# A row-wise LSTM behind a group norm: the second row's first products moved into the statistics, and the rest of it merged with the first row of the other half

## The chip, the cores and the metric

The kernel runs on one core of one Trainium2 chip. A core has five engines that each work through a queue of their own in order and wait for one another by semaphores: TensorE (PE in the profile, its weight loads PEld), VectorE (DVE), ScalarE (ACT), GpSimd (POOL) and SyncE (SP), which issues the transfers here. The metric is the time of one launch on the device in microseconds (us), taken as the median over several runs.

## The reference

The input `x` is an image batch of shape (8, 96, 128, 128): 8 images, 96 channels, 128 rows of 128 columns. It is normalised by group norm, 32 groups of 3 channels, with a mean and a variance over a whole image. A masked convolution of width 3 along each row gives 384 gate inputs. Then an LSTM runs down the 128 rows, where the state of a row is itself convolved along the columns:

```python
xn  = gn(x)                                    # mean and variance per image and group
its = conv1x3(xn, W_is * mask) + b_is          # for all rows
for row in range(128):
    gates = conv3(h, W_ss) + b_ss + its[row]
    f, i, o, g = sigmoid, sigmoid, sigmoid, tanh of the gates' quarters
    c = f * c + i * g
    h = o * tanh(c)
    out[row] = x[row] + h
```

The state before the first row is zero, so the first row needs no forget gate.

## The kernel before

**Two stages.** First the statistics: `x` is streamed through a ring of six buffers, image by image, six loads of 1 MB for each and 24 pieces of 512 columns in all. VectorE takes the statistics of most pieces (`bn_stats`, line 741), ScalarE sums the others with two activations each (lines 216 and 217). A table `events` says what else is queued after which piece: `at(6, 17)` is after the piece with number 17 of image 6. Then comes the recurrence, which nothing but the order of the rows binds.

**Halves and half-steps.** The batch is cut in two halves of four images, s = 0 and s = 1, so that one half's matmuls cover the other's gates. A half-step n handles row n // 2 of half n % 2; half-step 0 is row 0 of the first half, 1 is row 0 of the second, 2 is row 1 of the first. The images of the first half are scaled when their statistics are in, at `at(4, 5)`; half-step 0 runs inside the statistics of images 5 and 6. The second half's last image ends the statistics, so half-step 1 can begin only after them.

**One half-step.** Even and odd columns are kept apart, and the products are arranged so that the two outputs come out of sums and differences. The three gate tiles A, B and C have a bank of the matmul accumulator each (`ps`), two halves of 256 columns in it. The names in the order tables mean:

- `1` and `2`: matmuls of 128 contracted rows with the sum `vs` and the difference `vf` of the state's columns; `0` and `3`: the same with `vd`, the shifted differences
- `P`, `Q`, `E` (method `own`): matmuls of 64 contracted rows with the row's own image channels `xs`. The operands lie twice, in partitions 0 to 63 and 64 to 127; `low` picks one, by gate tile
- `cp` copies the first half of the bank with the bias added (`m`, lines 424 and 426); `lo` and `hi` write sum and difference back into the bank (lines 429 and 433). `E` and `0` then add to the first half, `3` to the second
- `ta`, `si`: tanh and sigmoid on ScalarE (lines 436 and 443); `fg`, `gt`, `ce`, `th`, `ou`: forget product, gate product, cell sum, tanh of the cell, output (lines 448, 452, 461, 466, 473)
- `F`, `S` on VectorE (lines 490 and 486) and `D` on GpSimd (line 494) make `vf`, `vs` and `vd` of the next row; `re` adds the output to `x` on GpSimd (line 512)

All matmuls of a half-step stand at line 380. A mark behind a name shifts it: `'` is the half-step before, `+` the next, `*` the one after that.

**What sets the order.** Every engine's queue is written out by hand. `do(n, names)` issues the named parts in order; `PERIOD` and `PRODUCTS` are the order of a half-step in the long run. `finish(n)` issues what comes up for later rows: own images of the next four rows (`own_image`, lines 292, 310 and 311 on GpSimd), shared channels (`normalise_shared`), loads of rows (`load_rows`, `load`) and stores. For half-steps 0 to 7 the list `FIRST` says which. Eight banks of the accumulator go round in the order of their request (`bank`), and a request waits until the last reader of the bank it gets is done.

**Fillers.** `spin(count, rhs)` issues matmuls whose result nobody reads, into a bank of their own; `keep_warm(count)` is one small one, tied to a piece of the statistics, and `count` more. `Scale` turns statistics into scale and shift by small matmuls (line 246) and a polynomial on VectorE; the second half has two, one for three images and one for the last (`late[1]`), each with two banks, `dm` and `pv`.

Behind the statistics, lines 746 to 786 scale the last image and make `vs`, `vf` and `vd` of half-step 1, then rows 1 to 3 of the second half's own images (`rows`, made by GpSimd one row after the other). The end of it and the start of the long run:

```python
    do(1, "1A 2A 1B 2B PA PB QA QB PC P+A QC")
    for n in range(1, last + 1):
        for names in PERIOD if n < last else PERIOD[:1]:
            do(n, PRODUCTS[n % 2] if names == "X" else names)
```

Of the kernel before, what the change touches and what calls it, by code (L numbers as in the profile page):

```python
# [21 lines left out]
def kernel(  # L22
# [34 lines left out]
    P = 128  # L57
    NH = 2
# [112 lines left out]
    def spin(count, rhs):  # L171
        unread = bank("spin")
        for i in range(count):
            nc.tensor.matmul(
                unread[:, 0 : rhs.shape[1]],
                wt[0][:, 0:P],
                rhs,
                start=True,
                stop=True,
                skip_group_check=True,  # L180
            )
# [44 lines left out]
    class Scale:  # L226


        def __init__(self, s, lo, hi):
            n, self.name = hi - lo, f"{s}_{lo}"  # L230
            self.st, self.rstd, self.nmr = (
                st[s][:, lo:hi], rstd[s][:, :, lo:hi], nmr[s][:, :, lo:hi]
            )

            self.dm = bank(f"dm{self.name}")[:, 0 : 3 * n].rearrange("p (i b) -> p i b", i=3)
            self.pv = bank(f"pv{self.name}")[:, 0 : 2 * n].rearrange("p (i b) -> p i b", i=2)
            self.pm = self.dm[:, 1:3, :]
            self.q, self.t, self.minus = (
                const.tile([P, *shape], F32, name=f"{name}{self.name}")
                for name, shape in (("q", [n]), ("t", [2, n]), ("minus", [2, n]))  # L240
            )
            for i in range(2):
                self.mm(self.pv[:, i, :], i, eps[:, 0:n], start=i == 0)

# [3 lines left out]
        def deviations(self):  # L248
            self.mm(self.dm[:, 0, :], 2, self.st[:, :, 0], start=True)

# [106 lines left out]
    class HalfStep:  # L357


        def __init__(self, n):  # L360
            self.row, self.s = divmod(n, NH)
            self.ps, self.m1, self.moving, self.done, self.gates = {}, {}, {}, set(), None
            self.hx = hx[self.s][self.row // R % 2][:, self.row % R]
            self.xs = xs[self.s][self.row // R % 2][:, self.row % R]
            self.c = cs[self.s].rearrange("p t b j -> p (t b j)")
# [5 lines left out]
        def g(self):  # L371
            if self.gates is None:
                self.gates = self.tile("g")
            return self.gates

        def mm(self, a, half, weights, rhs, rows=slice(0, P)):
            new = a not in self.ps
            if new:
                self.ps[a] = bank(f"ps{a}_{self.s}_{self.row}")
            nc.tensor.matmul(  # L380
                self.ps[a][:, bass.ts(half, HB)],
                weights[rows, bass.ts(a, P)],
                rhs[rows],
                start=new,
                stop=False,
                skip_group_check=True,
            )

        def own(self, a, i):

            low = a == order["A"] or (a == order["C"] and self.s == 0)
            rhs = self.xs[:, i].rearrange("p b j -> p (b j)")
            self.mm(a, i % 2, wo[i], rhs, slice(0, C2) if low else slice(C2, P))
# [26 lines left out]
        def copy(self, a):  # L420
            self.m1[a] = self.tile(f"m{a}", (P, HB))
            m1, column = self.ps[a][:, 0:HB], bias[:, a : a + 1]
            if a == order["A"] and self.row + self.s > 0:
                nc.vector.tensor_scalar(self.m1[a], m1, column, None, ALU.add)
            else:
                nc.scalar.activation(self.m1[a], m1, AF.Identity, bias=column)  # L426
# [101 lines left out]
    def shared(s, k, *images):  # L528
        return [(normalise_shared, nc.gpsimd, s, k, j, 0, R) for j in images]

    FIRST = [
        own(0, 0) + shared(0, 1, 0),
        own(0, 1, 2),
        own(0, 3) + [(load_rows, 0, 2)] + shared(0, 1, 1),
        own(1, 0, 1),
        own(1, 2) + shared(0, 1, 2, 3),
        own(1, 3) + [(load_rows, 1, 2)] + shared(1, 1, 0, 1),
        [(own_image, 0, 2, 0)] + shared(1, 1, 2, 3),
        [(own_image, 1, 2, 0)],
    ]  # L540
# [124 lines left out]

    def begin_scale(s, lo, hi):
        late.insert(0, Scale(s, lo, hi))
        late[0].deviations()
        late[0].variances(late[0].st[:, :, 1])
# [6 lines left out]
    def keep_warm(count):  # L676
# [7 lines left out]
        at(3, 21): lambda: first_rows(0, (2,)),  # L684
        at(4, 5): lambda: begin_scale(0, 0, BH),
        at(4, 6): squares,
# [9 lines left out]
        at(6, 8): lambda: (do(0, "gt th ou"), operands(2), do(0, "re")),  # L696
        at(6, 22): lambda: first_rows(1),
        at(7, 5): lambda: (late.insert(0, Scale(1, BH - 1, BH)), begin_scale(1, 0, BH - 1)),
        at(6, 17): lambda: keep_warm(13),
        at(7, 7): squares,  # L700
# [71 lines left out]
    step.total(lo=BH - 1)  # L772
    step.difference(lo=BH - 1)
    widen(nc.scalar, xw[1], BH - 1, 1, 1, 0, BH - 1, 0)
    own_row(xw[1], 1, 0, BH - 1, BH)
# [12 lines left out]

    do(1, "1A 2A 1B 2B PA PB QA QB PC P+A QC")
    for n in range(1, last + 1):  # L790
        for names in PERIOD if n < last else PERIOD[:1]:
            do(n, PRODUCTS[n % 2] if names == "X" else names)
            if "re'" in names.split():
                finish(n - 1)
# [66 lines left out]
```

## Time and profile before

| what | value |
|---|---|
| median of 4 runs | 2067.07 us (2066.55 to 2067.77) |
| profiled execution | 2065.83 us, its span 2064.0 us |
| busy: PE, DVE, ACT, POOL | 95%, 81%, 66%, 70% of the span |
| granted clock of TensorE, mean | 0.996 |
| matmuls at line 380, 128 rows: mean of one | 380 to 388 ns |
| copies (L426), sums (L429), differences (L433): mean of one | 474, 424, 429 ns |
| own images on POOL: L292, L311: mean of one | 806, 1062 ns |
| last input statistics on VectorE end | 132.4 us |

The page gives the busy time of each engine, then the span in 40 slices with a digit for each (tenths of the slice), then the chain of work that ended last, followed back from the end. Groups and timelines give the engine, the line, the operation, what it writes from what it reads, and in brackets how long the engine was idle before and what ended that. An f32 matmul shows as two records. The number in the clock's column is the share of full speed that TensorE was granted.

### The profile page before, as it was taken

Reading aid. Unit: us, or ns where it says so; the run is one execution under the profiler, and the core shown is the slowest. Engines: PE = TensorE matmul, PEld = TensorE weight load, DVE = VectorE, ACT = ScalarE, POOL = GpSimd, SP = SyncE. Lnnn points to the kernel's source line nnn. Section 1 sums busy time; section 2 is a strip of 40 time slices with the busy share of each in tenths; the row PEclk is TensorE's granted clock in tenths of the full one; section 3 lists DMA queues with packets and bytes.
Section 4 is the critical chain, followed back from the end, with each engine's and each line's share of the span. In section 5 each row is a group of like instructions: output and inputs, shape, how many; then the busy total and the mean of one; then the engine's idle time right before and its main releaser. Section 6 shows DMA issues by size and latency. Waiting matters only on the chain.

```text
span 2064.0 us, 31433 instructions
## 1 busy us (share of the span) xinstructions
PE 1961.5 (95%) x10880; PEld 1598.1 (77%) x10880; DVE 1677.8 (81%) x3490; ACT 1362.3 (66%) x2402; POOL 1446.3 (70%) x1652
## 2 busy tenths in 40 slices
PE   0389999999999999999999999999999999999998
PEld 0268888888888888888888888888888888888886
DVE  5768888888888888888888888888888888888887
ACT  4776666666666666666666666666666666666666
POOL 3358777777777777777777777777777777777762
PEclk9989999999999999999999999999999999999999
DMA  9994333444333344433334443333444333344411
GB/s 384 424 308 103 77 85 86 112 112 113 93 77 85 87 110 113 113 93 77 86 86 110 113 113 93 77 87 87 108 112 113 95 75 88 87 107 113 113 31 31
DMA packets 103325, 236.26 MB, mean 114 GB/s; under 512 B 5952, under 2 KB 8896, under 8 KB 97280
## 3 DMA queue, kind: packets, MB, share of 16 engines
q1 hardware_dynamic: 103168, 234.25, 41.2%
q8 instruction: 88, 1.44, 0.3%
q14 instruction: 69, 0.57, 0.1%
HBM read 183.90 MB, written 50.33 MB: 113 GB/s over the span
## 4 chain that ended last, share of the span: by engine, by line
PE 93%; DMA 3%; DVE 2%; ACT 1%; POOL 0%; issue 0%; SPq 0%; DVEq 0%; POOLq 0%
PE ps L380 93%; DMA xs<-in_x_dram 3%; DVE bst L741 1%; POOL xw L292 0%; POOL xs L311 0%; SPq L729 0%; POOL xs L310 0%; ACT piece L216 0%; ACT xs L216 0%; ACT xs L217 0%; ACT piece L217 0%; ACT g L436 0%; DVE st L664 0%; ACT th L466 0%; ACT ps L443 0%
## 5 line engine op out<-in xcount | busy, mean ns | idle before, releaser
L380 PE MATMUL ps<-vd,wl 128*128 128x256 f32 x3072 | 815.1, 388 | 0.0
L436 ACT ACTIVATE g<-ps 32x512 f32<-32x512 f32 x768 | 453.7, 591 | 453.4 <-PE ps L380 445.1
L380 PEld LDWEIGHTS ps<-vd,wl 128*128 128x128 f32 x3072 | 562.4, 190 | 151.2 <-issue 85.2
L494 POOL TENSOR_TENSOR vd<-hx 128x512 f32<-128x512 f32 x257 | 266.2, 1036 | 468.1 <-DVE vs L486 463.9
L380 PE MATMUL ps<-xs,wx 64*128 64x256 f32 x3072 | 457.7, 394 | 10.7 <-POOL xs L310 10.7
L380 PE MATMUL ps<-vs,wm 128*128 128x256 f32 x1536 | 458.6, 380 | 0.2 <-DVE vf L490 0.2
L380 PE MATMUL ps<-vf,wm 128*128 128x256 f32 x1536 | 458.2, 380 | 0.0
L443 ACT ACTIVATE ps<-ps 96x512 f32<-96x512 f32 x766 | 417.5, 572 | 16.2
L380 PEld LDWEIGHTS ps<-xs,wx 64*128 64x128 f32 x3072 | 322.8, 187 | 119.0 <-issue 84.2
L448 DVE TENSOR_TENSOR ps<-ps,c 96x512 f32<-96x512 f32 x254 | 176.8, 696 | 260.9 <-ACT ps L443 260.9
L433 DVE TENSOR_TENSOR ps<-m,ps 128x256 f32<-128x256 f32 x768 | 329.5, 429 | 26.4
L512 POOL TENSOR_TENSOR x<-x,hx 96x512 f32<-96x512 f32 x255 | 330.1, 1294 | 5.7 <-DVE hx L473 5.7
L429 DVE TENSOR_TENSOR ps<-m,ps 128x256 f32<-128x256 f32 x768 | 325.7, 424 | 10.0 <-ACT m L426 1.2
L380 PEld LDWEIGHTS ps<-vs,wm 128*128 128x128 f32 x1536 | 292.4, 191 | 41.3 <-POOL vs L486 0.7
L380 PEld LDWEIGHTS ps<-vf,wm 128*128 128x128 f32 x1536 | 292.6, 191 | 40.4 <-DVE vf L490 0.3
L426 ACT ACTIVATE m<-ps,wl 128x256 f32<-128x256 f32 x513 | 243.2, 474 | 76.2 <-PE ps L380 62.5
L311 POOL TENSOR_TENSOR xs<-xw 128x512 f32<-128x512 f32 (+1 forms) x254 | 269.7, 1062 | 0.0
L380 PE MATMUL ps<-xs,wt 64*128 64x256 f32 x1530 | 263.3, 376 | 0.0
L466 ACT ACTIVATE th<-c 96x512 f32<-96x512 f32 (+1 forms) x257 | 161.4, 628 | 105.1 <-DVE c L461 104.3
L292 POOL TENSOR_SCALAR hx<-x,rstd,nmr 32x512 f32<-32x512 f32 (+1 forms) x252 | 203.7, 808 | 26.0
L380 PEld LDWEIGHTS ps<-xs,wt 64*128 64x128 f32 x1530 | 194.4, 187 | 18.0 <-issue 0.7
L292 POOL TENSOR_SCALAR xw<-xr,rstd,nmr 128x512 f32<-128x512 f32 x252 | 203.2, 806 | 7.1 <-DVE nmr L284 6.6
(91 smaller groups left out, 1303.3 us busy)
## 6 DMA issues: line engine op xcount, KB each, us to landing
xr<-in_x_dram SPq DMA_DIRECT2D x124, 512.0 KB, 6.4
x<-in_x_dram SPq DMA_DIRECT2D x63, 768.0 KB, 5.9
out_dram<-x SPq DMA_DIRECT2D x62, 768.0 KB, 4.6
xs<-in_x_dram SPq DMA_DIRECT2D x30, 1024.0 KB, 12.3
piece<-in_x_dram SPq DMA_DIRECT2D x16, 1024.0 KB, 12.3
x<-in_x_dram SPq DMA_DIRECT2D x62, 256.0 KB, 3.2
xs<-in_x_dram SPq DMA_DIRECT2D x4, 512.0 KB, 8.2
out_dram<-x SPq DMA_DIRECT2D x2, 576.0 KB, 3.8
```

The lines of the kernel that those rows point to most:

```text
L292: engine.tensor_scalar(dst, src, scale, shift, ALU.mult, ALU.add)
L311: nc.gpsimd.tensor_sub(differences, strided(xw[:, 0, :], 0, [(W + 1, n), (J, 2), (1, J)]), strided(xw[:, 0, :], J + 1, [(W + 1, n), (0, 2) ...
L380: nc.tensor.matmul(self.ps[a][:, bass.ts(half, HB)], weights[rows, bass.ts(a, P)], rhs[rows], start=new, stop=False, skip_group_check=True,)
L426: nc.scalar.activation(self.m1[a], m1, AF.Identity, bias=column)
L429: nc.vector.tensor_add(self.ps[a][:, 0:HB], self.m1[a], self.ps[a][:, HB:])
L433: nc.vector.tensor_sub(hi, self.m1[a], hi)
L436: nc.scalar.activation(self.g[a * 32 : (a + 1) * 32], self.ps[a][C:P], AF.Tanh)
L443: nc.scalar.activation(gate, gate, AF.Sigmoid)
L448: nc.vector.tensor_mul(f, f, self.c)
L466: nc.scalar.activation(self.part(self.th, lo, hi), self.part(self.c, lo, hi), AF.Tanh)
L494: diff = nc.gpsimd.tensor_sub(self.operand("vd", 2)[:, :, lo:hi], strided(h, 1, [(BH * JP - 1, 2), (JP, hi - lo), (1, J)]), strided(h, 0, ...
L512: (nc.gpsimd if 2 * row + s < last else nc.vector).tensor_add(xo, xo, self.h)
```

## The change

Half-step 2 (row 1 of the first half) is taken apart.

- Its products `P`, `Q`, `1` and `2` for all gate tiles are issued at a new event `at(6, 9)`, inside the statistics, and its three copies on ScalarE at `at(6, 22)`. Its sums and differences `lo` and `hi` are issued on VectorE behind the last image's scaling.
- What is left of it (`E`, `0`, `3`, gates, output) is merged with half-step 1: the 64-row matmuls of both, and the first ones of half-step 3, form one phase in which the low and the high operands alternate; then come `0` and `3` of half-step 1, then those of half-step 2. For half-step 1, `hi` is issued behind `E`. The long run begins at half-step 3.
- `at(6, 17)` has 6 filler matmuls instead of 13. Fillers use a bank of half-step 1, which is requested early (`take_bank`), and the two `Scale` objects of the second half share one pair of banks and are created at `at(6, 9)`.
- For half-step 1, `low` of gate tile C's `E` is changed, and half-step 2's copy of tile A is done on ScalarE.
- `FIRST` is dealt out anew: the shared channels and the third block's loads and images come one half-step later or so.

```diff
@@ -169,7 +169,7 @@
     def spin(count, rhs):
-        unread = bank("spin")
+        unread = half_step(1).ps[0]
         for i in range(count):
             nc.tensor.matmul(
                 unread[:, 0 : rhs.shape[1]],
@@ -226,27 +226,32 @@
     class Scale:
-        def __init__(self, s, lo, hi):
+        def __init__(self, s, lo, hi, banks=None):
             n, self.name = hi - lo, f"{s}_{lo}"
             self.st, self.rstd, self.nmr = (
                 st[s][:, lo:hi], rstd[s][:, :, lo:hi], nmr[s][:, :, lo:hi]
             )
-            self.dm = bank(f"dm{self.name}")[:, 0 : 3 * n].rearrange("p (i b) -> p i b", i=3)
-            self.pv = bank(f"pv{self.name}")[:, 0 : 2 * n].rearrange("p (i b) -> p i b", i=2)
+
+            self.first, at = banks is None, 0 if banks is None else 3 * BH
+            self.banks = banks or [bank(f"{name}{self.name}") for name in ("dm", "pv")]
+            self.dm, self.pv = (
+                own[:, at : at + i * n].rearrange("p (i b) -> p i b", i=i)
+                for own, i in zip(self.banks, (3, 2))
+            )
             self.pm = self.dm[:, 1:3, :]
             self.q, self.t, self.minus = (
                 const.tile([P, *shape], F32, name=f"{name}{self.name}")
                 for name, shape in (("q", [n]), ("t", [2, n]), ("minus", [2, n]))
             )
             for i in range(2):
-                self.mm(self.pv[:, i, :], i, eps[:, 0:n], start=i == 0)
+                self.mm(self.pv[:, i, :], i, eps[:, 0:n], start=self.first and i == 0)
         def mm(self, o, i, rhs, start=False, stop=False):
             nc.tensor.matmul(o, gm[:, i, :], rhs, start=start, stop=stop, skip_group_check=True)
         def deviations(self):
-            self.mm(self.dm[:, 0, :], 2, self.st[:, :, 0], start=True)
+            self.mm(self.dm[:, 0, :], 2, self.st[:, :, 0], start=self.first)
         def variances(self, of):
             for i in range(2):
@@ -358,8 +363,9 @@
         def __init__(self, n):
-            self.row, self.s = divmod(n, NH)
+            self.n, (self.row, self.s) = n, divmod(n, NH)
             self.ps, self.m1, self.moving, self.done, self.gates = {}, {}, {}, set(), None
+            self.started = set()
             self.hx = hx[self.s][self.row // R % 2][:, self.row % R]
             self.xs = xs[self.s][self.row // R % 2][:, self.row % R]
             self.c = cs[self.s].rearrange("p t b j -> p (t b j)")
@@ -373,10 +379,14 @@
                 self.gates = self.tile("g")
             return self.gates
+        def take_bank(self, a):
+            if a not in self.ps:
+                self.ps[a] = bank(f"ps{a}_{self.s}_{self.row}")
+
         def mm(self, a, half, weights, rhs, rows=slice(0, P)):
-            new = a not in self.ps
-            if new:
-                self.ps[a] = bank(f"ps{a}_{self.s}_{self.row}")
+            self.take_bank(a)
+            new = a not in self.started
+            self.started.add(a)
             nc.tensor.matmul(
                 self.ps[a][:, bass.ts(half, HB)],
                 weights[rows, bass.ts(a, P)],
@@ -388,7 +398,7 @@
         def own(self, a, i):
-            low = a == order["A"] or (a == order["C"] and self.s == 0)
+            low = a == order["A"] or (a == order["C"] and (self.s == 0 or (self.n, i) == (1, 2)))
             rhs = self.xs[:, i].rearrange("p b j -> p (b j)")
             self.mm(a, i % 2, wo[i], rhs, slice(0, C2) if low else slice(C2, P))
@@ -420,7 +430,7 @@
         def copy(self, a):
             self.m1[a] = self.tile(f"m{a}", (P, HB))
             m1, column = self.ps[a][:, 0:HB], bias[:, a : a + 1]
-            if a == order["A"] and self.row + self.s > 0:
+            if a == order["A"] and self.n not in (0, 2):
                 nc.vector.tensor_scalar(self.m1[a], m1, column, None, ALU.add)
             else:
                 nc.scalar.activation(self.m1[a], m1, AF.Identity, bias=column)
@@ -529,14 +539,14 @@
         return [(normalise_shared, nc.gpsimd, s, k, j, 0, R) for j in images]
     FIRST = [
-        own(0, 0) + shared(0, 1, 0),
-        own(0, 1, 2),
-        own(0, 3) + [(load_rows, 0, 2)] + shared(0, 1, 1),
+        own(0, 0),
+        own(0, 1),
+        own(0, 2) + shared(0, 1, 0, 1),
+        own(0, 3) + [(load_rows, 0, 2)] + shared(0, 1, 2, 3),
         own(1, 0, 1),
-        own(1, 2) + shared(0, 1, 2, 3),
-        own(1, 3) + [(load_rows, 1, 2)] + shared(1, 1, 0, 1),
-        [(own_image, 0, 2, 0)] + shared(1, 1, 2, 3),
-        [(own_image, 1, 2, 0)],
+        own(1, 2) + shared(1, 1, 0, 1),
+        own(1, 3) + [(load_rows, 1, 2)] + shared(1, 1, 2, 3),
+        [(own_image, 0, 2, 0), (own_image, 1, 2, 0)],
     ]
     def work(n):
@@ -663,8 +673,16 @@
     def aggregate(b):
         nc.vector.bn_aggr(st[b // BH][:, b % BH, :], stats[b])
-    def begin_scale(s, lo, hi):
-        late.insert(0, Scale(s, lo, hi))
+    def next_products():
+
+
+        late[0:0] = [Scale(1, 0, BH - 1)]
+        late.insert(1, Scale(1, BH - 1, BH, late[0].banks))
+        for a in range(3):
+            half_step(1).take_bank(a)
+        do(2, "PA PB QA QB PC QC 1A 2A 1B 2B 1C 2C")
+
+    def begin_scale():
         late[0].deviations()
         late[0].variances(late[0].st[:, :, 1])
@@ -682,7 +700,7 @@
         at(3, 1): lambda: first_rows(0, (0,)),
         at(3, 13): lambda: first_rows(0, (1,)),
         at(3, 21): lambda: first_rows(0, (2,)),
-        at(4, 5): lambda: begin_scale(0, 0, BH),
+        at(4, 5): lambda: (late.insert(0, Scale(0, 0, BH)), begin_scale()),
         at(4, 6): squares,
         at(4, 8): lambda: (
             late[0].scale(), late[0].shift(), [own_image(0, 0, j) for j in range(BH)]
@@ -694,9 +712,10 @@
             0, "loA hiA EA 0A 3A loB hiB EB 0B 3B loC hiC EC 0C 3C taA taB siB taC siC"
         ),
         at(6, 8): lambda: (do(0, "gt th ou"), operands(2), do(0, "re")),
-        at(6, 22): lambda: first_rows(1),
-        at(7, 5): lambda: (late.insert(0, Scale(1, BH - 1, BH)), begin_scale(1, 0, BH - 1)),
-        at(6, 17): lambda: keep_warm(13),
+        at(6, 9): next_products,
+        at(6, 17): lambda: keep_warm(6),
+        at(6, 22): lambda: (first_rows(1), do(2, "cpA cpB cpC")),
+        at(7, 5): begin_scale,
         at(7, 7): squares,
         at(7, 8): lambda: (next_row(), spin(14, wt[0][:, 0:256])),
         at(7, 12): next_operands,
@@ -771,6 +790,7 @@
     step = half_step(1)
     step.total(lo=BH - 1)
     step.difference(lo=BH - 1)
+    do(2, "loA loC loB hiA hiB hiC")
     widen(nc.scalar, xw[1], BH - 1, 1, 1, 0, BH - 1, 0)
     own_row(xw[1], 1, 0, BH - 1, BH)
     step.shifted(BH - 1, BH)
@@ -786,8 +806,14 @@
     load_rows(1, 1)
-    do(1, "1A 2A 1B 2B PA PB QA QB PC P+A QC")
-    for n in range(1, last + 1):
+
+    do(1, "1A 2A 1B 2B 1C 2C PA PB QA QB E+A PC E+C QC P*A E+B cpA cpB cpC loA loB loC")
+    do(1, "EA P*B Q*A EB EC Q*B hiA hiB hiC 0A 3A 0B 3B 0C 3C taA taB siB taC siC")
+    finish(0)
+    do(1, "gt th 0+A 3+A 0+B 3+B 0+C 3+C ou F S D re")
+    finish(1)
+    do(2, "taA siA P+C P*A Q+C")
+    for n in range(3, last + 1):
         for names in PERIOD if n < last else PERIOD[:1]:
             do(n, PRODUCTS[n % 2] if names == "X" else names)
             if "re'" in names.split():
```

## The prediction, made before the changed kernel was run

> **What bounds the kernel now.** I read the page first (slices, then the chain that ended last), then the chain in order of time around the change, then each engine's timeline from 84 to 185 us. A "full" matmul below contracts 128 rows, a "half" one 64; the timeline counts two records for each.
>
> ```profile
> PE   0389999999999999999999999999999999999998
> PE 93%; DMA 3%; DVE 2%; ACT 1%; POOL 0%; issue 0%; SPq 0%; DVEq 0%; POOLq 0%
> ```
>
> From the third slice on TensorE is never free, and 93% of the span hangs on it. Whatever is taken out of TensorE's queue after the statistics shortens the kernel by its own length, if nothing then makes TensorE wait. The chain says where that stretch begins:
>
> ```profile
> 115.39 2.01 ACT xs L217 x2
> 117.42 11.21 DMA xs<-in_x_dram
> 128.65 3.79 DVE bst L741 x6
> ...
> 133.31 0.35 PE dm L246 x2
> ...
> 137.08 92.99 PE ps L380 x519
> ```
>
> Up to 137.08 the order is: ScalarE frees a buffer, the last load lands at 128.6, VectorE takes its statistics, the last image is scaled. From 137.08 it is matmuls alone. The unit prices stand in TensorE's timeline of the two rows after that:
>
> ```profile
> 137.08 0.67 PE L380 MATMUL ps<-vs,wm 128*128 128x256 f32 x2 [0.15 <-DVE vf L490]
> 138.98 2.00 PE L380 MATMUL ps<-xs,wx 64*128 64x256 f32 x14
> 140.91 0.70 PE L380 MATMUL ps<-vs,wm 128*128 128x256 f32 x2
> ...
> 145.19 0.70 PE L380 MATMUL ps<-vd,wl 128*128 128x256 f32 x2
> ...
> 150.57 1.57 PE L380 MATMUL ps<-xs,wx 64*128 64x256 f32 x12
> ...
> 153.46 0.59 PE L380 MATMUL ps<-vf,wm 128*128 128x256 f32 x2
> ...
> 160.77 0.59 PE L380 MATMUL ps<-vf,wm 128*128 128x256 f32 x2
> ```
>
> A full matmul starts every 0.433 us. The twelve between 145.19 and 150.57 take 5.38, so a run of full ones costs 0.433 each plus 0.18. Halves on opposite row halves run side by side: eight fill 143.26 to 145.19 (1.93) and ten fill 150.57 to 152.93 (2.36), so a run costs 0.433 per pair plus 0.2. Half-step 4 (third row of the first half) begins at 160.77, 23.69 us after 137.08. From half-step 4 on TensorE, ScalarE and VectorE have the same instructions in the same order and with the same waits before and after the change. So the question is how long those 23.69 us become, and whether 137.08 moves.
>
> **The change, part by part.**
>
> *Products of half-step 2 inside the statistics.* Six half and six full matmuls leave the stretch behind 137.08. The halves need row 1's own images, ready at 90.5, and start behind half-step 0's last matmul at 103.8. The full ones need `vs`, which GpSimd has ready at 110.47. At the slow pace that the timeline shows at 93.40 to 98.69 (0.86 each) they end by 115.7. The seven spins that go and the `eps` matmuls lay off the chain, on an engine that idled 8.8 us before them.
>
> *Copies on ScalarE.* Three of 0.47 us (group of L426) go behind the first rows, which end at 119.19. The next instruction waits 1.58 us for a load there:
>
> ```profile
> 120.77 0.20 ACT L215 ACTIVATE base<-xs 128x1 f32<-128x1 f32 x1 [1.58 <-DMA xs<-in_x_dram]
> ```
>
> 1.4 us fit into 1.58, and their matmuls are done 3.5 us earlier: cost 0. Without that cover each microsecond would delay the last image's sums and so 137.08. ScalarE's release of the last buffers (117.2) stands ahead of all this and stays.
>
> *Sums and differences on VectorE.* Six of 0.43 us move from between half-steps to 137.07, where VectorE idles 3.07 us until 140.14. At a pitch of 0.34 to 0.46 they end by 139.5: cost 0. Their reader, the `E` products of half-step 2, starts at 140.7.
>
> *The 64-row phase.* TensorE's new order behind 137.08, by the unit prices:
>
> - 6 full (half-step 1): 2.6 + 0.17 = 2.77, to 139.85
> - 16 halves, 8 pairs: 3.46 + 0.2 = 3.66, to 143.5 without a wait
> - 12 full (half-steps 1 and 2): 5.38
> - 3 halves, 2 slots: 1.07
> - 9 full (half-step 3): 3.9 + 0.17 = 4.07
> - 8 halves, then 1 full: 1.93 + 0.53
>
> Sum 19.4 against 23.69: 4.3 us at most. Now the waits that appear.
>
> First wait: the ninth half is the first product of half-step 3, which was at 150.57 and would now be at 139.85 + 4 x 0.433 = 141.6. It reads row 1's own images, which GpSimd makes with nothing free before them:
>
> ```profile
> 138.30 3.06 POOL L292 TENSOR_SCALAR hx<-x,rstd,nmr 32x384 f32<-32x384 f32 x4
> 141.44 0.64 POOL L310 TENSOR_TENSOR xs<-piece 128x256 f32<-128x256 f32 x1
> 142.04 1.06 POOL L311 TENSOR_TENSOR xs<-piece 128x512 f32<-128x512 f32 x1
> ```
>
> So it starts at 142.1 (+0.5), and the thirteenth, which needs L311, at 143.15 (+0.2). Behind it, in order, wait the `E` products of half-step 1, on which its differences on VectorE now wait (they were ahead of `E` before); these end at 143.6, 144.2 and 144.6, each ahead of its matmul. The 12 full ones start at 144.2 instead of 143.5: 0.7 lost.
>
> Second wait: half-step 3 needs half-step 1's output, through its gates. The sixth full matmul ends at 144.2 + 5 x 0.433 + 0.59 = 146.96; tanh 0.59 behind the sigmoid that ends at 147.3, the gate product 0.69, tanh 0.63, output 0.69 and difference 0.43, with 0.04 between each, end at 150.45. TensorE arrives at 144.2 + 5.38 + 1.07 = 150.65: no wait, with 0.2 to spare.
>
> Third wait: half-step 3 holds 9 full matmuls ahead of its halves where it held 11 and one more behind, because two of half-step 2's are done already. TensorE reaches half-step 4 after 4.07 + 1.93 + 0.53 = 6.53 us, at 157.2. VectorE's queue from its first copy to the difference took 154.53 to 160.53 = 6.0 us, of which the last 0.83 is a difference that took 0.43 elsewhere; now it starts at 151.65 and ends between 157.25 and 157.65. I take 157.3, since GpSimd has nothing to run at that moment. Later half-steps have 7.3 to 7.7 us each, so the lead is kept.
>
> 160.77 - 157.3 = 3.5 us gained.
>
> *Shared rows, images and loads put off by a half-step or so.* GpSimd waited 2.97 us at 152.76 and 0.76 at 161.01, and the busiest half-step now asks 1.04 + 1.29 + 5.1 = 7.4 of 7.5 us. The issues of the third block's rows on the sync queue go one half-step later, with some 30 us until the first reader. Cost 0; a block that came late would cost what TensorE then waits.
>
> *Does 137.08 move?* Earlier: no. VectorE's 1.0 us wait at 122.89 for TensorE goes, but a load ends its next wait at 126.15, and another lands at 128.6. Later: by the granted clock (the first number behind the five engines).
>
> ```profile
> 105.00:106.00 1.00, 0.00 (x0) 0.00 (x0) 1.00 (x3) 0.99 (x2) 0.00 (x0) 0.66 0.99 418
> 118.00:119.00 1.00, 1.00 (x4) 0.82 (x3) 0.92 (x3) 0.99 (x2) 0.00 (x0) 0.52 1.00 418
> 119.00:120.00 1.00, 1.00 (x6) 0.87 (x6) 1.00 (x3) 0.19 (x1) 0.00 (x0) 1.00 0.99 401
> ```
>
> It fell to a half some 1.5 us after the last matmul at 103.81 and came back 6.4 us after the spins began at 112.6. With six spins TensorE stops between 118.4 and 120.9 and waits until 121.35 for statistics; after a few tiny matmuls 14 spins start at 122.6. If the clock has dropped and stays down r us, they end at 128.7 + r/2, and 2.05 us of further filler must be through by 133.2. So r up to 5 costs nothing, 6.4 costs 0.7, and 9.0 (the ramp from 89.5 to 98.5) costs 2.0. I take 0.2, since a drop is likely but a long ramp is not.
>
> [...]
>
> **Sum.** -4.3 + 0.7 + 0.1 + 0.2 = -3.3 us. The profiled execution took 2065.83 (span 2064.0 and 1.83 around it), 1.24 below the median, so it would come to 2062.5 and the median of 2067.07 to 2063.8.
>
> **Rivals.**
> - *No wait appears.* If GpSimd's images or the clock come out better, the sum of prices holds: -4.3, 2062.8. For it: TensorE had no gap at all here before. Against: the GpSimd rows above.
> - *VectorE is late twice.* A difference can stretch: 1.06 at 174.75 beside a GpSimd instruction. At both places, less the 0.2 to spare, that costs 0.4 and 0.5 more, and with a 6.4 us ramp 0.7: -1.7, 2065.4. Against: GpSimd idles at both moments.
> - *The copies don't fit.* Then 137.08 moves as much as they overrun, at most 1.4: -1.9, 2065.2.
> - *The clock stays low (the slower side).* Place: the 14 spins. All at 0.86 end at 134.7, four more at 138.5, 5.3 us late: +2.0, 2069.1. From r = 12 us on the gain is gone; for over 0.2% slower it must also stay low for some 4 us of the long stretch. No ramp in this trace is that long.
>
> **How the numbers follow.** Chances: forecast (-2.5 to -4.0) 64%, no wait 14%, late VectorE or copies 16%, clock 6%. The predicted time is 2063.8; the range 2062.5 to 2065.7 spans the first three, with half a microsecond for the scatter of the median, and leaves out the clock and their edges. 0.2% is 4.1 us, about what a measurement of this kernel can tell from no change: only the upper half of "no wait" and a rare scatter lie beyond it on the faster side (13%), the clock partly on the slower (4%), the rest within (83%).
>
> **What would show it.** Right: half-step 4's first matmul 3.3 to 3.7 us earlier against the start of the long stretch; in that stretch one wait of TensorE on L310's successor near 142 and nothing over 0.3 us else; ScalarE's three copies before 120.8. Wrong: the aggregate's matmul later than 133.3 with a clock of 0.50 behind 122, a wait on `vf` at half-step 3 or 4, or a GpSimd wait in half-steps 4 to 8.

## The result and the profile after

The changed kernel took 2064.73 us (median of 42 runs, 2062.67 to 2066.49); the kernel before, run beside it, 2066.76 (60 runs). The ratio is 0.9989, with a 95% interval of 0.9984 to 0.9993: some 2.3 us less, at least 1.4 and at most 3.3. That lies within 0.2% and inside the range given, 0.9 us above the predicted time. The profiled executions differ by 1.7 us of span (2064.0 before, 2062.3 after).

From the page of the changed kernel, its span, TensorE's slices and its granted clock by slices, and the chain's shares:

```profile
span 2062.3 us, 31403 instructions
PE   0389999999999999999999999999999999999998
PEclk9989999999999999999999999999999999999999
PE 94%; DMA 3%; DVE 1%; POOL 1%; ACT 0%; issue 0%; SPq 0%; DVEq 0%; POOLq 0%
```

What binds is the same. What differs is the end of the statistics, read in the chain of the changed kernel in order of time (start, length, engine and what it wrote):

```profile
121.19 0.53 DVE st L674
...
124.97 10.21 PE ps L174 x40
...
143.10 0.65 POOL xs L315
...
143.79 8.59 PE ps L390 x46
...
152.41 87.75 PE ps L390 x483
```

Before, the last load and VectorE's statistics led to the last image's scaling at 133.31. Now 40 records of fillers (L174) stand there, 10.21 us of them: work whose result nobody reads has become the critical path. VectorE's last statistics were ready at the same time in both, 133.16 before (the first line) and 133.23 now:

```profile
132.53 0.63 DVE L664 BATCH_NORM_AGGREGATE st<-bst 128x2 f32<-128x105 f32 x1
132.60 0.63 DVE L674 BATCH_NORM_AGGREGATE st<-bst 128x2 f32<-128x105 f32 x1
```

Further down GpSimd's image (L315) is on the chain, and from 143.79 on it is matmuls alone. TensorE's timeline of the changed kernel gives the same with the waits in brackets:

```profile
115.50 2.84 PE L174 MATMUL ps<-wl 128*128 128x256 f32 x12
121.85 0.56 PE L251 MATMUL dm<-st,wl 128*128 128x3 f32 x2 [3.52 <-DVE st L674]
...
124.83 8.17 PE L174 MATMUL ps<-wl 128*128 128x256 f32 x28
...
135.01 0.28 PE L251 MATMUL dm<-st,wl 128*128 128x1 f32 x2
...
138.71 0.67 PE L390 MATMUL ps<-vs,wm 128*128 128x256 f32 x2 [0.15 <-DVE vf L500]
...
143.79 0.48 PE L390 MATMUL ps<-xs,wx 64*128 64x256 f32 x1 [0.33 <-POOL xs L315]
...
145.88 5.45 PE L390 MATMUL ps<-vd,wl 128*128 128x256 f32 x24
...
152.41 0.70 PE L390 MATMUL ps<-vf,wm 128*128 128x256 f32 x2
...
159.16 0.59 PE L390 MATMUL ps<-vf,wm 128*128 128x256 f32 x2
```

Three numbers carry the result. The long stretch starts at 138.71 instead of 137.08 (+1.63). Half-step 4 follows 20.45 us later instead of 23.69 (-3.24). From half-step 4 to the end of the span it is 1903.1 instead of 1903.2 (-0.1). The sum is -1.7, the difference of the spans.

### The profile page after: what moved, and what is told of

Its sections match the earlier page's. It is cut to its first block, busy times and chain, and to the rows that moved or that the text cites. A ratio compares the mean times of both kernels' runs of the same rounds, so it can differ in the third digit from the quotient of the medians.

```text
span 2062.3 us, 31403 instructions
## 1 busy us (share of the span) xinstructions
PE 1961.0 (95%) x10866; PEld 1597.6 (77%) x10866; DVE 1676.6 (81%) x3489; ACT 1363.7 (66%) x2403; POOL 1450.5 (70%) x1652
## 4 chain that ended last, share of the span: by engine, by line
PE 94%; DMA 3%; DVE 1%; POOL 1%; ACT 0%; issue 0%; SPq 0%; DVEq 0%; POOLq 0%
PE ps L390 93%; DMA xs<-in_x_dram 3%; DVE bst L760 1%; PE ps L174 1%; POOL xs L315 0%; POOL xs L316 0%; POOL xw L297 0%; SPq L748 0%; POOL hx L297 0%; PE pv L251 0%; ACT xs L217 0%; ACT xs L216 0%; ACT g L446 0%; PE dm L251 0%; ACT ps L453 0%
## 5 line engine op out<-in xcount | busy, mean ns | idle before, releaser
L316 POOL TENSOR_TENSOR xs<-xw 128x512 f32<-128x512 f32 (+1 forms) x254 | 270.3, 1064 | 0.0
```

What stands on the lines that cost most here:

```text
L316: nc.gpsimd.tensor_sub(differences, strided(xw[:, 0, :], 0, [(W + 1, n), (J, 2), (1, J)]), strided(xw[:, 0, :], J + 1, [(W + 1, n), (0, 2) ...
```

## The experiments

Theory at the start: the stretch gained what was forecast, and the halved clock of TensorE took half of it back ahead of 138.71, because 14 fillers stand in TensorE's queue before the last image's matmuls. Rivals for the late start: the shared or re-ordered banks make TensorE wait; a load or VectorE is late. Rivals for the gain: the merged phase earns it, or the products moved into the statistics do.

All kernels in one table. "Start" is the first matmul of the long stretch; "behind statistics" is the start less the end of VectorE's last aggregate (L664, now L674), since that end differs between these executions (133.16 to 134.63); "stretch" is the time from the start to half-step 4, "rest" the span less half-step 4. The median stands with its ratio to the kernel before, run beside it.

| run | start | behind statistics | stretch | rest | median us | ratio (95%) |
|---|---|---|---|---|---|---|
| before | 137.08 | 3.92 | 23.69 | 1903.2 | 2066.76 | |
| after | 138.71 | 5.48 | 20.45 | 1903.1 | 2064.73 | 0.9989 (0.9984 to 0.9993) |
| e1_spins13 | 137.50 | 3.86 | 20.44 | 1903.1 | 2063.26 | 0.9985 (0.9976 to 0.9993) |
| e2_spin8 | 137.21 | 3.86 | 20.47 | 1903.3 | 2063.31 | 0.9986 (0.9977 to 0.9994) |
| e3_before_spins6 | 140.68 | 6.05 | 23.68 | 1903.2 | 2068.52 | 1.0009 (1.0000 to 1.0018) |
| e5_no_merge | 140.18 | 6.81 | 20.23 | 1903.2 | 2064.93 | 0.9991 (0.9982 to 1.0000) |
| e4_images_first | 138.67 | 5.20 | 20.65 | 1903.1 | 2065.0 | 0.9991 (0.9982 to 1.0000) |
| e14_images_spins13 | 137.82 | 4.22 | 20.65 | 1903.1 | 2063.36 | 0.9985 (0.9976 to 0.9994) |
| e51_no_merge_spins13 | 139.33 | 5.89 | 20.23 | 1903.2 | 2063.07 | 0.9982 (0.9973 to 0.9990) |
| e7_first_old | 137.54 | 4.38 | 20.44 | 1903.8 | 2063.83 | 0.9986 (0.9978 to 0.9995) |
| e9_no_merge_13_8 | 137.59 | 3.86 | 20.23 | 1903.2 | 2062.83 | 0.9987 (0.9978 to 0.9996) |
| e10_images_finish_late | 137.05 | 3.86 | 19.71 | 1903.7 | 2063.10 | 0.9987 (0.9978 to 0.9996) |

Everything but the last two columns is one profiled execution, and its time lies apart from the median: by -0.9 us (before, 2065.83), -0.7 (after), +0.9 (e3), +0.5 (e5), and +1.5 (e51, the longest of its runs, 2064.6). A start stands for that execution, not for the median.

### The late start: e1, e2, e3

e1 gives the changed kernel the 13 fillers of before:

```diff
-        at(6, 17): lambda: keep_warm(6),
+        at(6, 17): lambda: keep_warm(13),
```

> The changed kernel with 13 filler matmuls at at(6, 17), as before, instead of 6. Clock theory: TensorE stays busy until about 121.2 us, the granted clock stays at 1.00 through 121 to 133, the last image's first small matmul comes at 133.3 instead of 135.0, the long stretch begins at 137.1 instead of 138.7, and the time falls by 1.6 us against the changed kernel (about 4 us or 0.2% below the kernel before, ratio 0.998). Bank theory (the second Scale shares the banks of the first and so starts late): the long stretch still begins at 138.7 and the ratio stays at 0.999. Load theory (loads landed 0.4 us later): the same, 138.7.

TensorE's timeline of e1:

```profile
116.59 5.86 PE L174 MATMUL ps<-wl 128*128 128x256 f32 x26
122.47 0.35 PE L251 MATMUL dm<-st,wl 128*128 128x3 f32 x2
...
124.19 6.29 PE L174 MATMUL ps<-wl 128*128 128x256 f32 x28
...
133.70 0.38 PE L251 MATMUL dm<-st,wl 128*128 128x1 f32 x2 [0.60 <-DVE st L674]
...
137.50 0.67 PE L390 MATMUL ps<-vs,wm 128*128 128x256 f32 x2 [0.15 <-DVE vf L500]
```

No wait of 3.52 us, the 14 fillers in 6.29 instead of 8.17, and TensorE waits for VectorE again before the last image's matmul, as before the change. The start comes 1.2 us earlier, and 1.6 counted from the last statistics, which were ready 0.4 later here. The median is 1.5 lower: 9 of e1's 11 runs lie below 2063.55, and 2 of the changed kernel's 42. The banks are those of the changed kernel, so banks are not the cause.

e2 leaves the six fillers and the wait, and shortens the queue instead:

```diff
-        at(7, 8): lambda: (next_row(), spin(14, wt[0][:, 0:256])),
+        at(7, 8): lambda: (next_row(), spin(8, wt[0][:, 0:256])),
```

> The changed kernel with 8 filler matmuls at at(7, 8) instead of 14; the 6 at at(6, 17) stay. Clock theory, with the delay sitting in the length of the filler queue: the clock still halves near 122, but the fillers end by 130.5 and the statistics of the last image are again what TensorE waits for; the long stretch begins at 137.1 and the time is 1.6 us below the changed kernel (ratio 0.998). If the slow clock itself costs the time (small matmuls of the scaling at half pace), the stretch begins later than 138. Bank theory: 138.7, ratio 0.999.

TensorE's timeline of e2, and two of its windows of 1 us (the number behind the five engines is the granted clock):

```profile
121.77 0.56 PE L251 MATMUL dm<-st,wl 128*128 128x3 f32 x2 [4.30 <-DVE st L674]
...
124.75 6.49 PE L174 MATMUL ps<-wl 128*128 128x256 f32 x16
...
133.41 0.38 PE L251 MATMUL dm<-st,wl 128*128 128x1 f32 x2
...
137.21 0.67 PE L390 MATMUL ps<-vs,wm 128*128 128x256 f32 x2 [0.16 <-DVE vf L500]
```

```profile
123.00:124.00 1.00, 1.00 (x6) 1.00 (x6) 0.32 (x1) 1.00 (x3) 0.19 (x2) 0.50 1.00 426
130.00:131.00 1.00, 1.00 (x5) 0.86 (x4) 1.00 (x3) 0.97 (x3) 1.00 (x2) 0.80 0.10 41
```

The wait is there (4.30) and the clock stands at 0.50 even longer than in the changed kernel (10.24 us against 6.84), yet the start comes 1.5 us earlier than in the changed kernel, 3.86 behind the statistics as in e1. So the slow clock alone costs nothing here. It costs when 14 fillers at the slow pace are queued ahead of a matmul that is needed.

e3 puts the six fillers alone into the kernel before:

```diff
-        at(6, 17): lambda: keep_warm(13),
+        at(6, 17): lambda: keep_warm(6),
```

> The kernel before with 6 filler matmuls at at(6, 17) instead of 13, nothing else. Clock theory: the seven missing fillers alone delay the long stretch, from 137.1 to 138.5 or 139, and the kernel is 1.4 to 2 us slower than before (ratio 1.0008). Bank theory and load theory: no change (137.1, ratio 1.000), since banks and loads are those of before.

TensorE's timeline of e3, and VectorE's last aggregate:

```profile
123.19 0.56 PE L246 MATMUL dm<-st,wl 128*128 128x3 f32 x2 [3.46 <-DVE st L664]
...
126.17 8.80 PE L174 MATMUL spin<-wl 128*128 128x256 f32 x28
```

```profile
134.00 0.63 DVE L664 BATCH_NORM_AGGREGATE st<-bst 128x2 f32<-128x105 f32 x1
```

The start is 140.68 instead of 137.08, later than the 138.5 to 139 expected. Of these 3.6 us 1.47 are not the fillers' doing: in this execution the last statistics were ready at 134.63 instead of 133.16, and the piece of them that the first filler waits for was late already (114.20 instead of 112.63). The other 2.13 are: TensorE waits 3.46 us, and the 14 fillers take 8.80. The median is 1.8 to 2.1 us above the kernel before, though its interval just reaches no change. In the changed kernel the statistics are not late (133.23), so with e1, e2 and e3 the number of fillers, and no bank or load, made its start late.

### Which part of the gain is whose: e5, e51

e5 keeps the products of half-step 2 in the statistics and drops the merged phase:

```diff
-    do(1, "1A 2A 1B 2B 1C 2C PA PB QA QB E+A PC E+C QC P*A E+B cpA cpB cpC loA loB loC")
...
-    do(2, "taA siA P+C P*A Q+C")
-    for n in range(3, last + 1):
+    do(1, "1A 2A 1B 2B PA PB QA QB PC QC")
+    for n in range(1, last + 1):
```

> The changed kernel without the merged phase: half-step 2's products, copies, sums and differences stay inside the statistics, but the order behind them is that of before (half-step 1 begins, then the long run from half-step 1 on, which skips what is done). By my unit prices the stretch up to half-step 4 is 1.9 + 1.93 + 2.35 + 1.07 + 2.77 + 2.36 + 0.53 + 4.95 + 1.93 + 0.53 = 20.3 us, against 20.45 measured in the changed kernel: the merged phase earns nothing, because its own wait for GpSimd's images eats what it saves; ratio 0.999 as the changed kernel. If the merged phase is what makes the change pay (half-step 1's gates would be uncovered without it), the stretch is 22 us or more and the kernel is no faster than before (ratio 1.000).

```profile
140.18 0.67 PE L390 MATMUL ps<-vs,wm 128*128 128x256 f32 x2 [0.15 <-DVE vf L500]
...
160.41 0.59 PE L390 MATMUL ps<-vf,wm 128*128 128x256 f32 x2
```

The stretch is 20.23 us, 0.2 shorter than with the merged phase, and the medians cannot be told apart (2064.93 and 2064.73). The merged phase earns nothing as it stands. Its wait on GpSimd is part of that; what it would save without the wait shows in e10 below. All of the 3.2 us, and 0.2 more, come from what went into the statistics (the new list, which e5 keeps, leaves the stretch as it is: see e7).

e51 is e5 with 13 fillers:

```diff
-        at(6, 17): lambda: keep_warm(6),
+        at(6, 17): lambda: keep_warm(13),
```

> No merged phase and 13 fillers. If the merged phase earns nothing, the stretch is 20.2 us as without it before, the start is back at 137.1 to 137.5, and the time equals that of the merged kernel with 13 fillers (2063.3, ratio 0.9985) or is 0.2 below it. If the merged phase is needed once the start is on time, it is slower than that by 0.5 us or more.

Its median is 1.9 us below e5's. In its profile 13 fillers were not enough:

```profile
114.51 5.86 PE L174 MATMUL ps<-wl 128*128 128x256 f32 x26
122.25 0.35 PE L251 MATMUL dm<-st,wl 128*128 128x3 f32 x2 [1.88 <-DVE st L674]
...
124.32 9.30 PE L174 MATMUL ps<-wl 128*128 128x256 f32 x28
```

The clock was back at full speed 3 us earlier than in e1 (113.36 and 116.34, from the last table), so the 13 ended at 120.4 instead of 122.45, TensorE waited 1.88 us, and the next 14 ran slowly: the start came 5.89 behind the statistics, 2.0 more than in e1. So 13 fillers help, but they do not make the start safe: e14 and e7, with 13 and 14 as well, lost 0.4 and 0.5 in the same way.

### The wait on GpSimd: e4, e14

e4 makes the images of row 1 before the shared channels of rows 1 to 3:

```diff
+    own_row(rows[:, 0:BH], 1, 1)
...
-    for r in range(1, R):
+    for r in range(2, R):
```

> The changed kernel, but GpSimd makes row 1's own images of the second half before the shared channels of rows 1 to 3 instead of after them; 6 fillers as in the change. GpSimd theory: the wait of 0.3 us (0.6 with the matmuls that it holds apart) in the 64-row phase goes, the stretch from the long stretch's first matmul to half-step 4 falls from 20.45 to about 19.8 us, and the time by 0.6 us against the changed kernel (2064.1 where that has 2064.7); the late start at 138.7 or more stays. If the phase is bound by something else (VectorE's sums, the gates of half-step 1), the stretch stays at 20.4.

The wait at 143.79 goes, and the 64-row phase ends 6.43 us after the start instead of 7.17. But the stretch is not shorter, 20.65 against 20.45. GpSimd's and VectorE's timelines of e4 and TensorE's:

```profile
150.81 0.64 POOL L315 TENSOR_TENSOR xs<-xw 128x256 f32<-128x256 f32 x1
151.41 1.25 POOL L316 TENSOR_TENSOR xs<-xw 128x512 f32<-128x512 f32 x1
```

```profile
151.14 0.58 DVE L500 TENSOR_TENSOR vf<-hx 128x256 f32<-128x256 f32 x1
151.65 1.28 DVE L496 TENSOR_TENSOR vs<-hx 128x256 f32<-128x256 f32 x1
```

```profile
151.78 0.70 PE L390 MATMUL ps<-vf,wm 128*128 128x256 f32 x2 [0.18 <-DVE vf L500]
...
152.99 0.70 PE L390 MATMUL ps<-vs,wm 128*128 128x256 f32 x2 [0.51 <-DVE vs L496]
```

With 0.7 us less in the phase, half-step 3 comes when GpSimd still works on an own image. The sum `vs`, 0.42 in the changed kernel, took 1.28 (and L316 1.25, 1.07 there), and TensorE waited 0.18 and 0.51. `vf`, 0.58 instead of 0.42, ends at 151.72, 0.27 behind L315 (151.45), and `vs` at 152.93, 0.27 behind L316 (152.66). The gain was lost to the two engines standing in each other's way; e10 below takes GpSimd's work away from there.

e14 is e4 with 13 fillers (the edits of e4 and e1 together):

> Both repairs: 13 fillers and row 1's own images first. If the two losses are independent, start 137.1 to 137.5 and stretch 19.8 add up to 2062.7 us, 0.6 below the run with 13 fillers alone (ratio 0.9982); if the second is hidden behind the gates of half-step 1, it stays at 2063.3 (0.9985).

Stretch 20.65 again, median 2063.36 against e1's 2063.26: so the order of GpSimd's work is worth nothing by itself, and the fillers are worth as much as in e1.

### What was costed at nothing: e7

e7 is e1 with the list `FIRST` of before:

```diff
-        own(0, 0),
-        own(0, 1),
-        own(0, 2) + shared(0, 1, 0, 1),
-        own(0, 3) + [(load_rows, 0, 2)] + shared(0, 1, 2, 3),
+        own(0, 0) + shared(0, 1, 0),
+        own(0, 1, 2),
+        own(0, 3) + [(load_rows, 0, 2)] + shared(0, 1, 1),
...
```

> The changed kernel with 13 fillers and with the list FIRST of the kernel before, so that shared channels, the third block's loads and its images come up at the old half-steps. My working put the new dealing at nothing: same time as with 13 fillers alone (2063.3, ratio 0.9985). If the merged phase needs GpSimd's queue cleared, TensorE waits for vd of half-step 3 or 4 and the time is 0.5 to 2 us higher.

The stretch is the same as in e1, the rest 0.76 us longer. VectorE's timeline of e7, at half-steps 4 and 6:

```profile
157.73 0.86 DVE L496 TENSOR_TENSOR vs<-hx 128x256 f32<-128x256 f32 x1
...
172.75 1.29 DVE L496 TENSOR_TENSOR vs<-hx 128x256 f32<-128x256 f32 x1
```

These half-steps took 8.08 and 8.13 us instead of some 7.7. With the old list GpSimd has an own image under way there, as in e4: L315 from 157.51 to 158.31, and L316 from 172.50 to 173.75. The trace shows 0.7 us for the new list; the medians (2063.83 and 2063.26) do not tell them apart.

### Putting it together: e9, e10

e9 is e51 with 8 instead of 14 fillers at `at(7, 8)`. e10 is e14 with the same, and with GpSimd's own images for later rows put behind half-step 1's outputs:

```diff
-    finish(0)
     do(1, "gt th 0+A 3+A 0+B 3+B 0+C 3+C ou F S D re")
+    finish(0)
```

> No merged phase, 13 fillers at at(6, 17) and 8 instead of 14 at at(7, 8). The profiled run with 13 and 14 had 1.9 us of idling after the 13, a clock of a half from 123.5 and fillers until 133.5, so 13 alone does not make the start safe. If what delays the start is only the queue of fillers in front of the last image's matmuls, a shorter second queue holds the start at 137.1 to 137.6 whatever the clock does, the stretch stays 20.2, and the scatter shrinks: median 2062.7, 0.3 below the run with 13 and 14 (ratio 0.9981). If a slow clock costs time of its own, the median stays at 2063.1.

> The merged phase with row 1's own images first, 13 and 8 fillers, and the images of half-step 0's finish queued on GpSimd behind half-step 1's output, so that nothing runs on GpSimd while VectorE makes vf and vs of half-step 3. Contention theory (in the run with images first, vs took 1.28 us instead of 0.42 beside GpSimd's L316, and TensorE waited 0.2 and 0.5 us for vf and vs): both waits go, vs takes 0.42 again, the stretch falls from 20.65 to 19.8 us and the median to 2062.3 (ratio 0.9979). If vs is slow for another reason, the stretch stays above 20.4.

e10's VectorE and TensorE:

```profile
149.52 0.42 DVE L500 TENSOR_TENSOR vf<-hx 128x256 f32<-128x256 f32 x1
149.87 0.42 DVE L496 TENSOR_TENSOR vs<-hx 128x256 f32<-128x256 f32 x1
```

```profile
137.05 0.67 PE L390 MATMUL ps<-vs,wm 128*128 128x256 f32 x2 [0.15 <-DVE vf L500]
...
156.76 0.59 PE L390 MATMUL ps<-vf,wm 128*128 128x256 f32 x2
157.43 0.70 PE L390 MATMUL ps<-vs,wm 128*128 128x256 f32 x2
...
164.84 0.59 PE L390 MATMUL ps<-vf,wm 128*128 128x256 f32 x2
```

With GpSimd idle beside them (2.12 us, until 150.43) `vf` and `vs` take 0.42 again, and the stretch is 19.71, the shortest of all. The work that was put off then meets the next sum: beside L315 (156.26 to 157.09) `vs` of half-step 4 takes 0.86, its matmul comes 0.67 behind `vf`'s instead of 0.43, that half-step takes 8.08 instead of e1's 7.73, half-step 7 takes 7.64 instead of the 7.34 of the changed kernel, and the rest is 0.6 us longer. The 2062.3 expected of e10 was met by its profiled execution (2062.31), but not by its median. The stretch is also 0.5 shorter than without the merged phase (20.23 in e5, e51 and e9): that is what the phase saves when nothing waits in it. In e9 the start is at 137.59, 3.86 behind the statistics, and the stretch 20.23, both as expected; the smaller scatter that was expected too did not appear.

Several runs of e9, e10 and the kernel before beside them were 2 to 6 us longer than their median; why stays open. The medians of e1, e2, e14, e51, e9 and e10 lie between 2062.83 and 2063.36. Each is 1.4 to 1.9 us below the changed kernel's median and 3.1 to 3.7 below that of the kernel before, run beside it, but they cannot be told apart from one another. The kernel before also moved between these groups (2066.41 to 2066.76): by the ratios the distance to the changed kernel is only 0.4 to 1.4 us, and the intervals overlap. What sets these kernels apart from it is the start in the traces, together with the runs. The simplest is e2's or e1's one number.

## Why the prediction held, and where it was wrong

**The number.** The time lies 0.9 us above the forecast and inside the range, but the gain was 2.0 us between the medians where 3.3 were forecast. That the time looks nearer than the gain is luck: the forecast set out from the median of four runs, 2067.07, and 60 runs gave 2066.76. Its own signs were mixed. Of those for being right, half-step 4 came 3.24 us earlier against the start (3.3 to 3.7 said), the wait of TensorE on GpSimd's image came as said, and ScalarE's copies ended at 120.85 (120.8 said); but the first sign of being wrong came too, the last image's matmul later than 133.3, at 135.01, with a clock of 0.50 behind 122.

**The prices of the stretch (-4.3).** Right but for 0.3. e10, where no wait is left in the stretch, took 19.71 for the forecast 19.4. The 0.3 stand where runs of full and half matmuls change: in the changed kernel the nine full ones before half-step 4 took 4.18 (forecast 4.07), the eight halves 2.04 (1.93) and the three before half-step 3 1.16 (1.07).

**First wait (+0.7).** Right in place, cause and size. The bracket shows 0.33 for L315 at 143.79, the phase ended 7.17 us after the start (forecast 7.12), and without the wait it ends at 6.43 (e4). The second wait did not appear, as forecast.

**Third wait (+0.1).** None: `vf` of half-step 4 has no bracket. The 6.75 us of that half-step (forecast 6.53) are TensorE's own. But the rival behind it, VectorE late beside GpSimd, was nearer than its 16% tell: 0.7 us less in the 64-row phase brought it about in e4, and the old list did in e7.

**Copies and sums at no cost.** Right. ScalarE's three copies ended at 120.85, and its next instruction waited 0.29 for its load, where it had waited 1.58:

```profile
119.64 1.21 ACT L436 ACTIVATE m<-ps,wl 128x256 f32<-128x256 f32 x3
121.14 0.20 ACT L215 ACTIVATE base<-xs 128x1 f32<-128x1 f32 x1 [0.29 <-DMA xs<-in_x_dram]
```

**The new list at no cost.** Right against the kernel before (1903.1 and 1903.2 from half-step 4 on), but it is no idle part: e7's trace shows that it keeps 0.7 us from being lost.

**"Does 137.08 move?" (+0.2).** This term was far too small: the start moved by 1.63 in the profile, 0.07 of it because the last statistics came later. The mechanism was named, and the size was off. The 14 fillers were put at 122.6 and began at 124.83: the statistics came at 121.85 (121.35 forecast), and the small matmuls of the scaling, put at 1.25 us, took 2.98. At full clock they take 1.72 (e1), and the trace of the kernel before had shown that: there they run from 122.49 to the fillers at 124.22. The slow clock made the other 1.26. From there even fillers at full pace (6.1 us) and the 2.05 us of further filler would have been through only at 132.98, 0.2 ahead of the 133.2 at which the last image's matmul was needed; the forecast had counted on 2.45 to spare. The slow pace then made 8.01 of the 6.1, and 1.7 of these 1.9 came through. VectorE's timeline shows it as a wait:

```profile
135.33 0.28 DVE L272 TENSOR_SCALAR q<-dm,st 128x1 f32<-128x1 f32 x1 [2.10 <-PE dm L251]
```

In sum: forecast -4.3 + 0.7 + 0.1 + 0.2 = -3.3; found in the traces -3.24 + 1.63 - 0.1 = -1.7, and -2.0 between the medians. The chances for "within 0.2%" rested on a gain of 2.5 to 4.0; it came out lower, at 2.0, still on the same side.

**The clock.** The forecast took the fall 1.5 us after the last matmul, the 6.4 us behind the spins' start and the 9.0 us of slow pace as times of their own. In the traces the turns lie in steps of 3.41 us (last section): the fall at 105.32 and the rise at 118.96 are 13.64 apart, four of them. Of the 9.0 us the first 3.9 were 64-row matmuls; the full ones began at 93.40, and 98.5, where the forecast saw their pace quicken (up to 97.83 they start 0.85 apart, and the two from 99.31 on take 1.13 together), lies two steps ahead of the fall at 105.32. (The clock's column shows 1.00 throughout there, so that ramp can be read from the pace alone.) A drop was called likely and a long ramp not. The drop came, and the clock stayed down for 6.84 us in the changed kernel (below), but for 10.24 in e2, e3 and e5. Nor did a fall need a whole step without full-size matmuls: they had filled 37% of the one at whose end e14's came.

The windows of 1 us in the changed kernel show where the clock turned:

```profile
121.00:122.00 1.00, 0.15 (x1) 0.18 (x2) 1.00 (x3) 0.82 (x2) 0.00 (x0) 0.91 1.03 434
122.00:123.00 1.00, 1.00 (x6) 1.00 (x6) 0.78 (x4) 0.97 (x3) 0.28 (x2) 0.50 0.99 418
...
128.00:129.00 1.00, 1.00 (x5) 0.86 (x4) 0.77 (x2) 0.93 (x3) 0.27 (x1) 0.67 1.01 406
129.00:130.00 1.00, 1.00 (x6) 0.90 (x5) 1.00 (x3) 0.97 (x2) 0.52 (x3) 1.00 0.52 205
```

0.91 is a fall 0.82 into its microsecond (0.18 of it at a half), 0.67 a rise 0.66 into its own: 121.82 and 128.66, 6.84 apart.

## What to carry to other kernels

Fillers that keep a clock up stand in the same queue as the work that they serve: count them at the slow pace too (14 took 8.17 us here instead of 6.29), and ask what waits behind them. Work taken off the bound engine paid most of its length here: in e5, where nothing was merged, 3.5 us of the 3.9 or so that six full and six half matmuls come to by the unit prices of the forecast. A gain further on, in e4 and e10, was used up by the next pair of engines that met. Where a step is costed at "a likely small thing", work it through at both paces, the small instructions in front of it included.

## What the runs showed of the hardware

The clock's turns in these profiles lie on a grid. Read off windows of 1 us as above, between 100 and 135 us:

| run | falls and rises, us |
|---|---|
| before | fall 105.32, rise 118.96 |
| after | fall 108.16, rise 115.00, fall 121.82, rise 128.66 |
| e3_before_spins6 | fall 107.38, rise 117.62, fall 121.02, rise 131.26 |
| e5_no_merge | fall 110.80, rise 114.20, fall 121.04, rise 131.28 |
| e2_spin8 | fall 109.92, rise 113.34, fall 120.16, rise 130.40 |
| e51_no_merge_spins13 | fall 109.94, rise 113.36, fall 123.60, rise 130.42 |
| e14_images_spins13 | fall 108.36, rise 115.18, fall 125.42, rise 128.84 |
| e1_spins13 | fall 109.50, rise 116.34 |
| e4_images_first | fall 109.16, rise 116.00, fall 122.82, rise 129.64 |
| e7_first_old | fall 107.58, rise 114.40, fall 124.64, rise 128.06 |
| e9_no_merge_13_8 | fall 109.50, rise 116.32 |
| e10_images_finish_late | fall 107.44, rise 114.28, fall 124.52, rise 127.92 |

Every distance between two neighbouring turns of a row is 1, 2, 3 or 4 times 3.41 us, to 0.03, and where the grid lies differs from execution to execution. The changed kernel and e5 are the same program up to 138 us, with the same fillers: there the last rise came at 128.66 and 131.28, and the start 5.48 and 6.81 behind the statistics, where 3.86 is what it takes without a queue of fillers in the way. So what the halved clock costs is no fixed number, and one profile shows one draw of it. How much of the scatter of the changed kernel's runs (2062.67 to 2066.49) this makes was not measured.

"Full-size" is a matmul of 128 rows and 256 columns here. In these profiles a rise came only at the end of a grid step that such matmuls filled to 87% or more (e3's first is the emptiest); in e51 and e5 they filled 79% of the step before the last rise's, and the clock stayed down. Matmuls of 3 columns between two runs of fillers did not always keep it up: e51, with 1.88 us of waiting and 2.1 us of them, fell, e14 fell with 0.94 and 1.7, and e9, with 0.33 and 1.7, did not. From which share of a step a fall follows stays open: e9 kept the clock through a step with full-size matmuls in 46% of it, and e14 lost it with 37%. The length of a gap alone did not decide: 2.66 us between two full-size matmuls, all but 0.53 of it in one step, cost e14 the clock (121.48 to 124.14), and the same 2.66, cut 1.84 to 0.82 by the grid, did not cost it in e9 (128.14 to 130.80).
